# Third stage of a convolution block: quarter-array passes first, then full-row passes, in each chunk

## The chip, the cores and the metric

The kernel runs on one core of one Trainium2 chip. The metric is the device time of one execution in microseconds (us). Five engines work side by side, each through its own instruction list in order: TensorE (PE in the profile; its weight loads are PEld), VectorE (DVE), ScalarE (ACT), GpSimd (POOL) and SyncE (SP). Here SP and POOL mostly issue DMAs. All data is fp32.

## The reference, cut to what matters

The input x is 16 images of 192 channels, 64 x 64 pixels. The work that this change touches is the last third of the first layer:

```python
mixed = gelu(batch_norm((scanned + local) * sigmoid(gate)))     # BN statistics over all images
x  = x + conv1x1(mixed, out_proj_w, out_proj_b)                 # 192 -> 192
h2 = layer_norm_over_channels(x)                                # mean, variance, sqrt(var + 1e-6)
x  = x + conv1x1(gelu(conv1x1(h2, fc1_w, fc1_b)), fc2_w, fc2_b) # 192 -> 768 -> 192
```

Before it come a layer norm, an input projection, a depthwise convolution, and scans in four directions. After it, a second layer averages each image over its pixels, makes 3 x 3 masked depthwise taps from that average (four of the nine are used), and applies them to the image.

## The kernel before

The program has three stages. The first (layer norm and input projection) ends at about 630 us of the span, the second (convolution, scans, batch-norm statistics) at about 1300 us, and the third, which the change is about, takes the rest.

**Tiling of stage three.** Images go in pairs: image 2p on partitions 0 to 63, image 2p + 1 on partitions 64 to 127, so that the 192 channels of both are three tiles t = 0, 1, 2 of 64 channels each. A chunk is 512 pixels (8 rows) of one pair; there are 8 chunks a pair and n_ch = 64 chunks in all. Per chunk the steps are:

- `load`: x of the chunk into one of two buffers `x2s` (SP queue). `load_mixed`: every second chunk, `mixed` into `y_low` (SP queue). `unmix`: three DVE transposes of it into `mxs`. `bn_gelu`: batch norm and GELU on ACT.
- out-projection of tile t: `out_quarters` uses channels 128 to 191 of `mixed`, with quarters of the PE array (64 rows x 64 columns, four matmuls abreast); `out_columns` uses channels 0 to 127 with full rows (128 rows x 64 columns, two abreast). Both add up in one pair of PSUM areas. `residual` (DVE) adds it to x and writes the image `ximg`, and makes the channel sums `sm`.
- layer norm: `mean(n, ..., "sm")` on quarters of the array, `center` (DVE), `squares` (ACT and DVE), `mean(n, ..., "sq")` on quarters, which is the variance, and `normalize`: Sqrt on ACT, reciprocal and multiply on DVE. An ACT table has to be loaded for Sqrt and again for GELU (`warm`).
- `first`: the 192 to 768 product on quarters of the array, six tiles m of 128 outputs, each followed by a GELU on ACT into a `gl` tile. `second`: the 768 to 192 product with full rows (through the helper `both`, so its line in the profile is that of the helper). `final` (DVE) adds it to the image and sums over pixels.
- `piece`: one part of the second layer for the pair before (`dynamic`): one ACT pass, three DVE passes, two output DMAs on the POOL queue. 12 pieces a pair, at most two a chunk. `pooled`, `squeeze` and `excite` compute the taps once a pair.

**Order.** `tc.manual_schedule` keeps each engine's instructions in the order in which the code issues them, so the order of calls is the schedule. A chunk before has three rounds k = 0, 1, 2: `first(n, k)` with two tiles m, then `products(n, k)`, then one `second`. `products(n, t)` puts a mean of chunk n + 1 (t = 0: mean, t = 1: variance) and one tile t of the out-projection of chunk n + 2 into one PSUM tile. On PE a round is therefore: quarters (first, mean, out_quarters), then full rows (out_columns, second).

**PSUM.** Of eight banks, tag "f1" has two buffers of two banks (first, and the out-projection with the means), tag "f2" three buffers of one bank (the three outputs of second), tag "a" one bank.

**Lines of the profile.** L989 is first's matmul and L991 its GELU; L843 is second's matmul (and excite's); L907 is out_quarters, L914 out_columns, L945 mean, L920 residual, L957 center, L964 and L965 squares, L973 to L977 normalize, L1009 final, L1046 and L65 a piece, L870 and L871 bn_gelu, L243 unmix, L1074 a pass of the tail. The end of the kernel (the last pair's second layer) is written out after the loop and shares tags with it (`ol` tiles have the tag "gl").

Of the kernel before, what the change touches and what calls it, by code (L numbers as in the profile page):

```python
# [55 lines left out]
def conv_block_kernel(ctx: ExitStack, tc: tile.TileContext, x, prm, w_in, w_out, w_fc1, b_fc1, w_fc2, w1, bn1, w2, out):  # L56
# [46 lines left out]
    w2t = k2.tile([RED, NTAP, C], F32, tag="w2t", name="w2t")  # L103
    b1 = k2.tile([RED, 4], F32, tag="b1", name="b1")
    s1 = k2.tile([RED, 1], F32, tag="s1", name="s1")
    pv = k2.tile([128, 2, NPRM], F32, tag="pv", name="pv")

    mean64 = k2.tile([128, 64], F32, tag="mean64", name="mean64")

# [55 lines left out]
    SB_ = 2 * 2 * C * BR  # L165
    mid = ce.tile([128, SB_], F32, tag="mid", name="mid")
    ones = ce.tile([128, 128], F32, tag="ones", name="ones")


    bias_g = ce.tile([128, C], F32, tag="bias_g", name="bias_g")  # L170
# [678 lines left out]
    def rows(a):  # L849
        return a.rearrange("p (h w) -> p h w", w=HW)  # L850

    def load(n):
        if n >= 2:
            load_x2(n)
        st[n].update(x2=x2s[n % 2])
# [6 lines left out]
    def unmix(n):  # L862

        for t in range(3 if n else 0):
            turn_back(ys[n // 2], mxs[n % 2], n % 2, t)
        st[n].update(mx=mxs[n % 2])
# [3 lines left out]
        nc.scalar.activation(mx[:, 0:2], mx[:, 0:2], AF.Gelu, bias=bn_bi[:, 0:1], scale=bn_sc[:, 0:1])  # L870
        nc.scalar.activation(mx[:, 2], mx[:, 2], AF.Gelu, bias=bn_bi[:, 1:2], scale=bn_sc[:, 1:2])  # L871

    def products(n, t):


        if not -2 <= n < n_ch - 1:
            return
        ps = ps2.tile([128, 2, CH], F32, tag="f1", name="ps_o", bufs=2)
        pm, po = ps[:, :, HCH:CH], [ps[:, wh, 0:HCH] for wh in range(2)]
        if t < 2:  # L880
            at(mean, n + 1, pm, ("sm", "sq")[t])
        at(out_proj, n + 2, t, po)

        if t == 0:
            at(center, n + 1, pm)
        if t == 1 and 0 <= n + 1 < n_ch:
            st[n + 1]["pw"] = pm
        at(residual, n + 2, t, po)

    cols = lambda a: a.rearrange("p r (k w) -> p r k w", k=2)  # L890

    def out_proj(n, t, ps):
# [6 lines left out]
            out_quarters(n, t, ps, True)  # L899
            out_columns(n, t, ps, False)  # L900

    def out_quarters(n, t, ps, first_):
        s = st[n]

        for wh, qr in enumerate(HALF):
            for i, q in enumerate(HALF):
                nc.tensor.matmul(ps[wh][q], wo2[qr, 64 * t:64 * t + 64], s["mx"][qr, 2, 256 * i:256 * i + 256],  # L907
                                 start=first_, stop=not first_)

    def out_columns(n, t, ps, first_):  # L910
        s = st[n]
        for wh in range(2):
            for i, q in enumerate(HALF):
                nc.tensor.matmul(ps[wh][q].rearrange("p (r w) -> p r w", w=32), wo[:, 64 * t:64 * t + 64],  # L914
                                 cols(rows(s["mx"][:, i]))[:, :, wh], start=first_, stop=not first_)

    def residual(n, t, ps):
        s, img = st[n], img_of(n)
# [20 lines left out]
    def mean(n, ps, what):  # L939


        s0, s1, sx = st[n][what]
        for k, kinds in enumerate(((s0, sx), (sx, s1))):
            for i, a in enumerate(kinds):
                nc.tensor.matmul(ps[HALF[i], k], mean64[HALF[k]], a[HALF[k]], start=True, stop=True)  # L945

    def mean_part(n, pm, t, k, src):

        for i, q in enumerate(HALF):
            nc.tensor.matmul(pm[q, k], mean64[q], src[q], start=(t == 0 and k == 0), stop=(t == 2 and k == 1))  # L950

    def center(n, pm):
        s, img = st[n], img_of(n)
        h = hp2.tile([128, 3, CH], F32, tag="h2", name="h2")
        hr = CR // 2
        for k in range(2):
            nc.vector.tensor_sub(h.rearrange("p t (h w) -> p t h w", w=HW)[:, :, k * hr:(k + 1) * hr], img[:, :, k * hr:(k + 1) * hr],  # L957
                                 rows(pm[:, k]).unsqueeze(1).broadcast_to([128, 3, hr, HW]))
        s.update(h=h)

    def squares(n):
        s = st[n]
        sq = wp.tile([128, 3, CH], F32, tag="sq2", name="sq2")
        nc.scalar.activation(sq, s["h"], AF.Square)  # L964
        nc.vector.tensor_add(sq[:, 0], sq[:, 0], sq[:, 1])  # L965
        v = sq.rearrange("p t (k n) -> p t k n", k=2)
        sums(v[:, 0, 0], v[:, 0, 1], v[:, 1, 0], v[:, 0, 0], v[:, 0, 1], v[:, 2, 0], v[:, 2, 1])
        s.update(sq=(v[:, 0, 0], v[:, 0, 1], v[:, 1, 0]))

    def normalize(n):  # L970
        s = st[n]
        rs = hp2.tile([128, CH], F32, tag="rs2", name="rs2", bufs=1)
        nc.scalar.activation(rs.rearrange("p (k n) -> p k n", k=2), s["pw"], AF.Sqrt, bias=eps6)  # L973

        nc.scalar.activation(warm, eps6, AF.Gelu)
        nc.vector.reciprocal(rs, rs)  # L976
        nc.vector.tensor_mul(s["h"], s["h"], rs.unsqueeze(1).broadcast_to([128, 3, CH]))  # L977

    def first(n, k):

        s = st[n]
        s["gl", k] = []
        for m in (2 * k, 2 * k + 1):
            pf = ps2.tile([128, 2, CH], F32, tag="f1", name="ps_f1", bufs=2)
            for t in range(3):
                for i, q in enumerate(HALF):
                    for j, o in enumerate(HALF):
                        m0 = 128 * m + 64 * j
                        nc.tensor.matmul(pf[o, i], wf1[q, t, m0:m0 + 64], s["h"][q, t], start=(t == 0), stop=(t == 2))  # L989
            gl = wp.tile([128, 2, CH], F32, tag="gl", name="gl", bufs=4)  # L990
            nc.scalar.activation(gl, pf, AF.Gelu, bias=bf1[:, m:m + 1])  # L991
            s["gl", k].append(gl)

    def second(n, k):
        s = st[n]
        if k == 0:
            s["po"] = [ps2.tile([128, CH], F32, tag="f2", name="ps_f2", bufs=3) for _ in range(3)]
        for j, gl in enumerate(s.pop(("gl", k))):
            m = 2 * k + j
            for t in range(3):  # L1000
                both(s["po"][t], lambda i: wf2[:, m, 64 * t:64 * t + 64], lambda i: gl[:, i], m == 0, m == NFC - 1)

# [49 lines left out]
    def dynamic_last(p, r, nr, t, dg, o=None, queues=(nc.gpsimd, nc.sync)):  # L1052
# [11 lines left out]
                nc.sync.dma_start(ov[2 * p + i, 64 * t:64 * t + 64, r * HW:(r + nr) * HW], o[HALF[i]].rearrange("p h w -> p (h w)"))  # L1064
            return

        o = wp.tile([128, GR, HW], F32, tag="gl", name="ol", bufs=4)
        ps = ps2.tile([128, 2, CH], F32, tag="f1", name="ps_d", bufs=2)[:, :, 0:hr * HW]
        for k in range(NTAP):
            for i, q in enumerate(HALF):  # L1070
# [10 lines left out]
    def at(f, n, *a):  # L1081
        if n is not None and 0 <= n < n_ch:
            f(n, *a)
# [3 lines left out]
    def piece():  # L1087
        if pieces:
            dynamic(*pieces.pop(0))

    def out_alone(n, t, later=False):

        if later:
            ps = [ps2.tile([128, CH], F32, tag="f2", name="ps_o2", bufs=3)[:, 0:HCH] for _ in range(2)]
        else:
            pair = ps2.tile([128, 2, CH], F32, tag="f1", name="ps_o", bufs=2)
            ps = [pair[:, wh, 0:HCH] for wh in range(2)]
        out_proj(n, t, ps)
        if not later:
            residual(n, t, ps)  # L1100
        return ps

    def one_bank():
        return ps2.tile([128, 2, HCH], F32, tag="a", name="ps_m")

    def idle(k):

# [20 lines left out]
    for k in range(2):  # L1128
        mean_part(0, pm, 2, k, img0[:, 2, halves[k]])
    center(0, pm)  # L1130
    load(2)
    sq0 = wp.tile([128, 3, CH], F32, tag="sq2", name="sq2").rearrange("p t (k n) -> p k t n", k=2)
    for k in range(2):
        nc.scalar.activation(sq0[:, k], st[0]["h"].rearrange("p t (k n) -> p k t n", k=2)[:, k], AF.Square)
    nc.scalar.activation(warm, eps6, AF.Sqrt)
# [2 lines left out]
    for k in range(2):  # L1138
        for t in range(3):
            mean_part(0, pw, t, k, sq0[:, k, t])  # L1140
    st[0]["pw"] = pw
    normalize(0)
    load_y(4, ys[2], (nc.gpsimd,))
    residual(1, 1, out_alone(1, 1, True))
    out_alone(1, 2)
    idle(1)
    first(0, 0)
    pm = ps2.tile([128, 2, CH], F32, tag="f1", name="ps_o", bufs=2)[:, :, 0:HCH]
    mean(1, pm, "sm")
    unmix(2)  # L1150
    center(1, pm)
    bn_gelu(2)
    squares(1)
    load(3)
    first(0, 1)
    unmix(3)
    out_alone(2, 0)
    second(0, 0)
    bn_gelu(3)
    products(0, 1)  # L1160
    normalize(1)
    first(0, 2)
    products(0, 2)
    second(0, 1)
    nc.vector.memset(pool2, 0.0)

    for n in range(1, n_ch + 1):
        ended = (n - 1) // NCH if n >= NCH and (n - 1) % NCH == NCH - 1 else None
        if n == 1:
            load_y(6, ys[3], (nc.gpsimd,))  # L1170
        if n == NCH - 3:
            border(ximg[1])
        at(load, n + 3)
        at(unmix, n + 3)
        at(load_mixed, n + 4)
        at(first, n, 0)
        at(bn_gelu, n + 3)
        products(n, 0)
        piece()
        at(squares, n + 1)  # L1180
        at(second, n - 1, NPS - 1)
        at(final, n - 1)
        if ended is not None:
            pooled(ended)
            if ended == n_pairs - 1:
                idle(1)
        at(first, n, 1)
        products(n, 1)
        if ended is not None:
            squeeze(ended)  # L1190
        at(second, n, 0)
        piece()
        at(normalize, n + 1)
        at(first, n, 2)
        if ended is not None:
            excite(ended)
            if ended < n_pairs - 1:
                pieces += [(ended, g, t) for g in range(NG) for t in range(3)]
        products(n, 2)
        at(second, n, 1)  # L1200

    last = n_pairs - 1

    def taps_on_diagonals(j):
# [73 lines left out]
```

## Time and profile before

| | us |
|---|---|
| median of 3 runs | 3713.8 (3713.1 to 3716.2) |
| profiled execution | 3712.9 |
| its span, first to last instruction | 3711.1 |
| PE busy | 3689.3 |
| DVE busy | 2702.0 |
| ACT busy | 1782.6 |
| POOL busy | 419.2 |

The profile is of one execution, whose own time lies 1.8 us above its span and 0.9 us below the median. Busy times are summed over the whole span. PE, PEld, DVE, ACT and POOL work side by side, so their times do not add up. A matmul's row in the trace has its true start and a modelled end; PE can look busy while it does not run at its peak. In the groups, `64*64` or `128*64` behind MATMUL is the part of the array (rows times columns) that one instruction takes.

### The profile page before, as it was taken

The page shows a single profiled execution, that of the slowest core. Times are in us where ns is not written, and L with a number is a line of the kernel's source. Part 1 is how long each engine was busy: PE and PEld are TensorE (multiplying, and loading weights), DVE is VectorE, ACT ScalarE, POOL GpSimd, SP SyncE. Part 2 cuts the span into 40 slices and gives each one's busy share as a digit, 9 for nine tenths or more (in the row PEclk, how much of TensorE's full clock was granted, in tenths as well). Part 3 has the DMA queues.
Part 4 walks back from the last instruction along what each step waited for, and adds up shares of the span by engine and source line. Part 5 has one row for each costly group of instructions (what it writes and reads, how often), then busy time and mean ns, then how long its engine had stood idle before and what let it go on. Part 6 is the DMA issues. An engine that isn't in the chain of part 4 may idle for free.

```text
span 3711.1 us, 71206 instructions
## 1 busy us (share of the span) xinstructions
PE 3689.3 (99%) x30354; PEld 1664.0 (45%) x30354; DVE 2702.0 (73%) x4138; ACT 1782.6 (48%) x1940; POOL 419.2 (11%) x685
## 2 busy tenths in 40 slices
PE   9999999999999999999999999999999999999998
PEld 6666666555555533333333333333333333333333
DVE  7878776999999965557656756766675766675764
ACT  3344344888888843334434343434343443443433
POOL 2434342111011020000000000000000000000000
PEclk9999999999999999999999999999999999999999
DMA  7898998999999851112212222222222221221212
GB/s 170 245 255 248 263 276 262 291 297 284 282 281 280 221 101 40 41 44 71 81 51 64 74 61 66 63 66 63 72 57 63 77 67 46 77 75 43 69 38 74
DMA packets 290332, 491.80 MB, mean 133 GB/s; under 512 B 26584, under 2 KB 184784, under 8 KB 290016
## 3 DMA queue, kind: packets, MB, share of 16 engines
q1 hardware_dynamic: 232540, 296.22, 29.7%
q0 software_dynamic: 56544, 189.99, 18.7%
q8 instruction: 240, 3.93, 0.5%
q10 hardware_dynamic: 932, 1.03, 0.1%
q14 instruction: 76, 0.62, 0.1%
HBM read 284.95 MB, written 197.92 MB: 130 GB/s over the span
## 4 chain that ended last, share of the span: by engine, by line
PE 90%; DMA 1%; DVE 1%; ACT 0%; issue 0%; ACTq 0%; SPq 0%; DVEq 0%
PE ps_f L989 27%; PE ps_f L843 27%; PE ps_l L673 11%; PE ps_pj L514 7%; PE ps_d L629 7%; PE ps_o L914 5%; PE ps_o L907 2%; PE ps_o L945 1%; PE ps_xt L485 1%; DMA xa<-in_x_dram 0%; PE ps_k L843 0%; DVE o L65 0%; PE pb_h L142 0%; PE ps_m L950 0%; DMA pg_d<-mid 0%; DVE ol L65 0%
## 5 line engine op out<-in xcount | busy, mean ns | idle before, releaser
L991 ACT ACTIVATE gl<-ps_f,bf 128x1024 f32<-128x1024 f32 x384 | 427.5, 1113 | 1319.5 <-PE ps_f L989 1319.5
L989 PE MATMUL ps_f<-h,wf 64*64 64x512 f32 x9216 | 1033.3, 593 | 3.0 <-DVE h L977 1.9
L843 PE MATMUL ps_f<-gl,place 128*64 128x512 f32 x4608 | 1022.2, 592 | 0.0
L989 PEld LDWEIGHTS ps_f<-h,wf 64*64 64x64 f32 x9216 | 333.6, 133 | 688.4 <-issue 633.7
L843 PEld LDWEIGHTS ps_f<-gl,place 128*64 128x64 f32 x4608 | 334.2, 137 | 574.5 <-issue 533.4
L514 PE MATMUL ps_pj<-wi,xa 64*128 64x384 f32 x3072 | 514.6, 487 | 0.6 <-DVE mid L519 0.3
L957 DVE TENSOR_TENSOR h<-ximg,ps_o 128x768 f32<-128x768 f32 x126 | 114.6, 951 | 420.6 <-PE ps_o L914 412.3
L514 PEld LDWEIGHTS ps_pj<-wi,xa 64*128 64x128 f32 x3072 | 292.0, 187 | 194.7 <-issue 10.6
L920 DVE SCALAR_TENSOR_TENSOR ximg<-ps_o,pt,low 128x256 f32<-128x256 f32 x384 | 167.9, 479 | 262.8 <-PE ps_o L914 260.3
L65 DVE SCALAR_TENSOR_TENSOR o<-ximg,taps,o 128x1024 f32<-128x1024 f32 (+1 forms) x267 | 337.5, 1264 | 11.2 <-ACT o L1046 2.6
L1050 POOL DMA_DIRECT2D out_dram<-o x168 | 89.8, 539 | 2065.7 <-DVE o L65 2062.9
L976 DVE RECIPROCAL rs<-rs 128x512 f32<-128x512 f32 x64 | 214.3, 3349 | 28.6 <-ACT rs L973 28.6
L664 DVE TENSOR_TENSOR_SCAN v<-tab,q 128x1024 f32<-128x1024 f32 x96 | 218.3, 2274 | 6.6 <-ACT tab L652 6.6
L666 DVE TENSOR_TENSOR_SCAN v<-tab,q 128x1024 f32<-128x1024 f32 x96 | 217.5, 2265 | 0.0
L652 ACT ACTIVATE tab<-mask,dec_b 128x1024 f32<-128x1024 f32 x192 | 209.5, 1143 | 0.0
L520 ACT ACTIVATE mid<-ps_pj,rsa 128x384 f32<-128x384 f32 x128 | 120.4, 942 | 183.5 <-PE ps_pj L514 183.5
L914 PE MATMUL ps_o<-low,wo 128*64 128x256 f32 x1536 | 208.1, 392 | 0.0
L520 ACT ACTIVATE stg<-ps_pj,rsa 128x384 f32<-128x384 f32 x128 | 120.2, 941 | 178.9 <-PE ps_pj L514 174.9
L492 DVE BATCH_NORM_STATS2 st<-ps_xt 128x6 f32<-128x192 f32 x512 | 173.3, 339 | 13.2 <-PE ps_xt L485 12.4
L243 DVE STREAM_TRANSPOSE low<-low 128x512 f32<-128x512 f32 x174 | 167.9, 1016 | 2.1 <-issue 0.3
L1009 DVE SCALAR_TENSOR_TENSOR ximg<-ps_f,pt,ximg 128x512 f32<-128x512 f32 x192 | 134.4, 748 | 40.2 <-PE ps_f L843 37.8
L473 POOL DMA_DIRECT2D xa<-in_x_dram x192 | 119.6, 631 | 358.9 <-PE ps_pj L514 317.9
(214 smaller groups left out, 4060.8 us busy)
## 6 DMA issues: line engine op xcount, KB each, us to landing
low<-in_x_dram SPq DMA_DIRECT2D x128, 384.0 KB
out_dram<-o POOLq DMA_DIRECT2D x168, 256.0 KB, 3.7
mid<-pg_d SPq DMA_DIRECT2D x8, 4096.0 KB
low<-mixed_d SPq DMA_DIRECT2D x116, 256.0 KB
low<-pg_d SPq DMA_DIRECT2D x7, 4096.0 KB
pg_o<-pg_d SPq DMA_DIRECT2D x7, 4096.0 KB
xa<-in_x_dram POOLq DMA_DIRECT2D x192, 128.0 KB, 5.5
xa<-in_x_dram SPq DMA_DIRECT2D x192, 128.0 KB
```

The source lines that it names most:

```text
L65: nc.vector.scalar_tensor_tensor(o, in0, scalar, in1, ALU.mult, ALU.add, **kw)
L514: nc.tensor.matmul(ps[i], pixels(n, t, g)[q], wi[q, t].rearrange("p g k c -> p (g k c)"), start=(t == 0), stop=(t == 2))
L520: nc.scalar.activation(stag[blk][1][:, :, j], ps[1], AF.Copy, scale=rs[:, g, 1:2])
L629: nc.tensor.matmul(dst(ps[o, ih]), mats[g % 2]["dm"][q, di + 1, :, ch], src(s["pg"][q, :, 0, ch]), start=(di == 0), stop=stop)
L664: nc.vector.tensor_tensor_scan(vf, tab, q, 0.0, ALU.mult, ALU.add)
L666: nc.vector.tensor_tensor_scan(vf[:, ::-1], tab[:, ::-1], q[:, ::-1], 0.0, ALU.mult, ALU.add)
L673: nc.tensor.matmul(dst(bst[k]["ps"][o, i]), lm_of(g)[q, m, :, c], src(q, ih), start=start, stop=stop)
L843: nc.tensor.matmul(ps[q], w(i), rhs(i), start=start, stop=stop)
L914: nc.tensor.matmul(ps[wh][q].rearrange("p (r w) -> p r w", w=32), wo[:, 64 * t:64 * t + 64], cols(rows(s["mx"][:, i]))[:, :, wh], start=fi ...
L976: nc.vector.reciprocal(rs, rs)
L989: nc.tensor.matmul(pf[o, i], wf1[q, t, m0:m0 + 64], s["h"][q, t], start=(t == 0), stop=(t == 2))
L991: nc.scalar.activation(gl, pf, AF.Gelu, bias=bf1[:, m:m + 1])
```

## The change

In stage three a chunk now has two phases on PE in place of three rounds. First all passes on quarters of the array: first(n, 0) and first(n, 1), the mean of chunk n + 1, first(n, 2) to first(n, 5), out_quarters of chunk n + 2 for t = 0 and 2, the variance of chunk n + 1, out_quarters for t = 1. Then those with full rows: out_columns for the three t, and second with all six tiles.

For this, `first` makes one tile m a call, `gl` has six buffers instead of four, `products` is gone, the out-projection's three outputs lie in two "f1" tiles taken together, and mean and variance take two buffers of "f2" each (so Sqrt is two instructions of 256 columns). `squares` writes into the x2 buffer of its chunk, and so `load` of chunk n + 3 is issued after the variance. `final(n - 1)` comes at the start of a chunk's code, `unmix`, `load_mixed` and the first `piece` behind the first calls, `normalize`, the residuals and `bn_gelu` after out_columns, the second `piece` inside second. `pv` moves to a pool that is closed before stage three.

```diff
-    def products(n, t):
-        if not -2 <= n < n_ch - 1:
-            return
-        ps = ps2.tile([128, 2, CH], F32, tag="f1", name="ps_o", bufs=2)
-        pm, po = ps[:, :, HCH:CH], [ps[:, wh, 0:HCH] for wh in range(2)]
-        if t < 2:
-            at(mean, n + 1, pm, ("sm", "sq")[t])
-        at(out_proj, n + 2, t, po)
-        if t == 0:
-            at(center, n + 1, pm)
-        if t == 1 and 0 <= n + 1 < n_ch:
-            st[n + 1]["pw"] = pm
-        at(residual, n + 2, t, po)
...
     def squares(n):
         s = st[n]
-        sq = wp.tile([128, 3, CH], F32, tag="sq2", name="sq2")
+        sq = x2s[n % 2]
...
-        nc.scalar.activation(rs.rearrange("p (k n) -> p k n", k=2), s["pw"], AF.Sqrt, bias=eps6)
+        for k in range(2):
+            nc.scalar.activation(rs[:, k * HCH:(k + 1) * HCH], s["pw"][k], AF.Sqrt, bias=eps6)
...
+    def two_banks(name):
+        return [ps2.tile([128, CH], F32, tag="f2", name=name, bufs=3)[:, 0:HCH] for _ in range(2)]
...
-    for n in range(1, n_ch + 1):
+    for n in range(n_ch + 1):
         ended = (n - 1) // NCH if n >= NCH and (n - 1) % NCH == NCH - 1 else None
-        at(load, n + 3)
-        at(unmix, n + 3)
-        at(load_mixed, n + 4)
-        at(first, n, 0)
-        at(bn_gelu, n + 3)
-        products(n, 0)
-        piece()
-        at(squares, n + 1)
-        at(second, n - 1, NPS - 1)
         at(final, n - 1)
...
+        at(first, n, 0)
         at(first, n, 1)
-        products(n, 1)
+        if n + 1 < n_ch:
+            pm = two_banks("ps_m")
+            mean(n + 1, pm, "sm")
+            center(n + 1, pm)
...
+        at(first, n, 2)
+        at(squares, n + 1)
+        for m in range(3, NFC):
+            at(first, n, m)
...
+        at(unmix, n + 3)
+        at(load_mixed, n + 4)
+        piece()
+        po = []
+        if n + 2 < n_ch:
+            pair = [ps2.tile([128, 2, CH], F32, tag="f1", name="ps_o", bufs=2) for _ in range(2)]
+            po = [[pair[j][:, wh, c0:c0 + HCH] for wh in range(2)] for j, c0 in ((0, 0), (1, 0), (0, HCH))]
+            for t in (0, 2):
+                out_quarters(n + 2, t, po[t], True, t < 2)
+        if n + 1 < n_ch:
+            st[n + 1]["pw"] = two_banks("ps_v")
+            mean(n + 1, st[n + 1]["pw"], "sq")
+        at(load, n + 3)
+        if n + 2 < n_ch:
+            out_quarters(n + 2, 1, po[1], True)
         if ended is not None:
             squeeze(ended)
+        for t in range(len(po)):
+            out_columns(n + 2, t, po[t], False, t > 0)
+        at(normalize, n + 1)
+        for t in range(len(po)):
+            residual(n + 2, t, po[t])
+        at(bn_gelu, n + 3)
         at(second, n, 0)
-        piece()
-        at(normalize, n + 1)
-        at(first, n, 2)
         if ended is not None:
             excite(ended)
...
-        products(n, 2)
         at(second, n, 1)
+        piece()
+        at(second, n, 2)
```

In the code that starts stage three, the passes that were written out for chunk 0 are now the loop's n = 0; there `unmix(2)` stands behind the first mean and `bn_gelu(2)` behind first(0, 4).

More of the change, by code (lines that the diff above doesn't have):

```diff
@@ L105, in conv_block_kernel @@
     s1 = k2.tile([RED, 1], F32, tag="s1", name="s1")
-    pv = k2.tile([128, 2, NPRM], F32, tag="pv", name="pv")
     mean64 = k2.tile([128, 64], F32, tag="mean64", name="mean64")
@@ L167, in conv_block_kernel @@
     ones = ce.tile([128, 128], F32, tag="ones", name="ones")
+    pv = ce.tile([128, 2, NPRM], F32, tag="pv", name="pv")
     bias_g = ce.tile([128, C], F32, tag="bias_g", name="bias_g")
@@ L900, in out_proj, with out_quarters @@
             out_columns(n, t, ps, False)
-    def out_quarters(n, t, ps, first_):
+    def out_quarters(n, t, ps, first_, start=None):
         s = st[n]
@@ L907, in out_quarters, with out_columns @@
                 nc.tensor.matmul(ps[wh][q], wo2[qr, 64 * t:64 * t + 64], s["mx"][qr, 2, 256 * i:256 * i + 256],
-                                 start=first_, stop=not first_)
-    def out_columns(n, t, ps, first_):
+                                 start=first_ if start is None else start, stop=not first_)
+    def out_columns(n, t, ps, first_, stop=None):
         s = st[n]
@@ L914, in out_columns @@
                 nc.tensor.matmul(ps[wh][q].rearrange("p (r w) -> p r w", w=32), wo[:, 64 * t:64 * t + 64],
-                                 cols(rows(s["mx"][:, i]))[:, :, wh], start=first_, stop=not first_)
+                                 cols(rows(s["mx"][:, i]))[:, :, wh], start=first_, stop=not first_ if stop is None else stop)
     def residual(n, t, ps):
@@ L944, in mean @@
             for i, a in enumerate(kinds):
-                nc.tensor.matmul(ps[HALF[i], k], mean64[HALF[k]], a[HALF[k]], start=True, stop=True)
+                nc.tensor.matmul(ps[k][HALF[i]], mean64[HALF[k]], a[HALF[k]], start=True, stop=True)
     def mean_part(n, pm, t, k, src):
         for i, q in enumerate(HALF):
-            nc.tensor.matmul(pm[q, k], mean64[q], src[q], start=(t == 0 and k == 0), stop=(t == 2 and k == 1))
+            nc.tensor.matmul(pm[k][q], mean64[q], src[q], start=(t == 0 and k == 0), stop=(t == 2 and k == 1))
     def center(n, pm):
@@ L957, in center @@
             nc.vector.tensor_sub(h.rearrange("p t (h w) -> p t h w", w=HW)[:, :, k * hr:(k + 1) * hr], img[:, :, k * hr:(k + 1) * hr],
-                                 rows(pm[:, k]).unsqueeze(1).broadcast_to([128, 3, hr, HW]))
+                                 rows(pm[k]).unsqueeze(1).broadcast_to([128, 3, hr, HW]))
         s.update(h=h)
@@ L977, in normalize, with first @@
         nc.vector.tensor_mul(s["h"], s["h"], rs.unsqueeze(1).broadcast_to([128, 3, CH]))
-    def first(n, k):
+    def first(n, m):
         s = st[n]
[L982 to L992, printed above, removed]
+        pf = ps2.tile([128, 2, CH], F32, tag="f1", name="ps_f1", bufs=2)
+        for t in range(3):
+            for i, q in enumerate(HALF):
+                for j, o in enumerate(HALF):
+                    m0 = 128 * m + 64 * j
+                    nc.tensor.matmul(pf[o, i], wf1[q, t, m0:m0 + 64], s["h"][q, t], start=(t == 0), stop=(t == 2))
+        gl = wp.tile([128, 2, CH], F32, tag="gl", name="gl", bufs=6)
+        nc.scalar.activation(gl, pf, AF.Gelu, bias=bf1[:, m:m + 1])
+        s["gl", m] = gl
     def second(n, k):
@@ L997, in second @@
             s["po"] = [ps2.tile([128, CH], F32, tag="f2", name="ps_f2", bufs=3) for _ in range(3)]
-        for j, gl in enumerate(s.pop(("gl", k))):
-            m = 2 * k + j
+        for m in (2 * k, 2 * k + 1):
+            gl = s.pop(("gl", m))
             for t in range(3):
@@ L1065, in dynamic_last @@
             return
-        o = wp.tile([128, GR, HW], F32, tag="gl", name="ol", bufs=4)
+        o = wp.tile([128, GR, HW], F32, tag="gl", name="ol", bufs=6)
         ps = ps2.tile([128, 2, CH], F32, tag="f1", name="ps_d", bufs=2)[:, :, 0:hr * HW]
@@ L1093, in out_alone @@
         if later:
-            ps = [ps2.tile([128, CH], F32, tag="f2", name="ps_o2", bufs=3)[:, 0:HCH] for _ in range(2)]
+            ps = two_banks("ps_o2")
         else:
@@ L1103, in one_bank @@
     def one_bank():
-        return ps2.tile([128, 2, HCH], F32, tag="a", name="ps_m")
+        ps = ps2.tile([128, 2, HCH], F32, tag="a", name="ps_m")
+        return [ps[:, k] for k in range(2)]
+    def two_banks(name):
+        return [ps2.tile([128, CH], F32, tag="f2", name=name, bufs=3)[:, 0:HCH] for _ in range(2)]
     def idle(k):
@@ L1130, in conv_block_kernel @@
     center(0, pm)
-    load(2)
-    sq0 = wp.tile([128, 3, CH], F32, tag="sq2", name="sq2").rearrange("p t (k n) -> p k t n", k=2)
+    sq0 = x2s[0].rearrange("p t (k n) -> p k t n", k=2)
     for k in range(2):
@@ L1141, in conv_block_kernel @@
     st[0]["pw"] = pw
+    load(2)
     normalize(0)
@@ L1146, in conv_block_kernel @@
     idle(1)
[L1147 to L1165, printed above, removed]
-    for n in range(1, n_ch + 1):
-        ended = (n - 1) // NCH if n >= NCH and (n - 1) % NCH == NCH - 1 else None
[L1169 to L1172, printed above, removed]
-        at(load, n + 3)
-        at(unmix, n + 3)
-        at(load_mixed, n + 4)
-        at(first, n, 0)
-        at(bn_gelu, n + 3)
-        products(n, 0)
-        piece()
-        at(squares, n + 1)
-        at(second, n - 1, NPS - 1)
+    for n in range(n_ch + 1):
+        ended = (n - 1) // NCH if n >= NCH and (n - 1) % NCH == NCH - 1 else None
         at(final, n - 1)
@@ L1186, in conv_block_kernel @@
                 idle(1)
-        at(first, n, 1)
-        products(n, 1)
+        if n == 0:
+            nc.vector.memset(pool2, 0.0)
+        if n == 1:
+            load_y(6, ys[3], (nc.gpsimd,))
+        if n == NCH - 3:
+            border(ximg[1])
+        at(first, n, 0)
+        at(first, n, 1)
+        if n + 1 < n_ch:
+            pm = two_banks("ps_m")
+            mean(n + 1, pm, "sm")
+            center(n + 1, pm)
+        if n == 0:
+            unmix(2)
+        at(first, n, 2)
+        at(squares, n + 1)
+        for m in range(3, NFC):
+            at(first, n, m)
+            if n == 0 and m == 4:
+                bn_gelu(2)
+        at(unmix, n + 3)
[13 more added lines that the diff above has]
+            out_quarters(n + 2, 1, po[1], True)
         if ended is not None:
             squeeze(ended)
+        for t in range(len(po)):
[4 more added lines that the diff above has]
+        at(bn_gelu, n + 3)
         at(second, n, 0)
-        piece()
-        at(normalize, n + 1)
-        at(first, n, 2)
         if ended is not None:
```

## The prediction

> **What bounds the kernel now.** I read the page first: busy times, the slices, the groups.
>
> ```profile
> span 3711.1 us, 71206 instructions
> PE 3689.3 (99%) x30354; PEld 1664.0 (45%) x30354; DVE 2702.0 (73%) x4138; ACT 1782.6 (48%) x1940; POOL 419.2 (11%) x685
> PEclk9999999999999999999999999999999999999999
> L976 DVE RECIPROCAL rs<-rs 128x512 f32<-128x512 f32 x64 | 214.3, 3349 | 28.6 <-ACT rs L973 28.6
> ```
>
> PE is busy all the time at full clock, DVE has a quarter free. But "busy" is not "at its peak", so the second view is the PE timeline of one chunk in the middle of stage three, with a first() block at both ends:
>
> ```profile
> 2303.43 5.38 PE L989 MATMUL ps_f<-h,wf 64*64 64x512 f32 x48
> 2308.63 0.61 PE L907 MATMUL ps_o<-low,wo 64*64 64x256 f32 x8
> 2309.17 1.08 PE L914 MATMUL ps_o<-low,wo 128*64 128x256 f32 x8
> 2310.08 5.32 PE L843 MATMUL ps_f<-gl,place 128*64 128x512 f32 x24
> 2315.33 5.38 PE L989 MATMUL ps_f<-h,wf 64*64 64x512 f32 x48
> 2320.53 0.61 PE L945 MATMUL ps_o<-sm,mean 64*64 64x256 f32 x8
> 2320.96 0.61 PE L907 MATMUL ps_o<-low,wo 64*64 64x256 f32 x8
> 2321.51 1.08 PE L914 MATMUL ps_o<-low,wo 128*64 128x256 f32 x8
> 2322.42 5.32 PE L843 MATMUL ps_f<-gl,place 128*64 128x512 f32 x24
> 2327.67 5.38 PE L989 MATMUL ps_f<-h,wf 64*64 64x512 f32 x48
> ...
> 2340.01 2.38 PE L989 MATMUL ps_f<-h,wf 64*64 64x512 f32 x20
> ```
>
> Columns: start, duration, engine, line, operation, tiles, rows\*columns of the array, count. Only the starts matter (ends are modelled). Four 64\*64 matmuls run abreast, or two 128\*64. In the weight-load rows of the first block, ten steps take 2303.91 to 2308.20: 0.429 us for a group of 512 columns; a group of 256 takes half, 0.215 (L945 to L907, two groups: 0.43). No block waits for data: the view of waits, for PE alone between 1400 and 3640 us, is empty. What the reader is to see is where the starts are later than the columns explain. L945 to L907, both 64\*64: nothing lost. L907 to L914, 64\*64 to 128\*64: 0.55 instead of 0.43. L914 to L843, both 128\*64: 0.91 instead of 0.86, 0.05 lost (in finer time behind its first pair, so it is the tail of the change before). L843 to L989, back: 5.25 instead of 5.15, and the L989 block itself 5.20. So a round trip from quarters to full rows and back loses about 0.12 + 0.05 + 0.10 + 0.05 = 0.32. Check on the whole chunk: 2303.43 to 2340.01 is 36.58 us; columns are 72 groups of 512 (30.91) and 22 of 256 (4.74), 35.65. The rest, 0.93, over three round trips is 0.31 each. I use 0.31.
>
> **The change, part by part.** *Round trips.* Each of the 64 chunks now has one in place of three: quarters for first(), both means and out_quarters, then full rows for out_columns and second(). Two saved: 2 x 0.31 x 64 = **-39.7 us**. The Trainium skill, "TensorEngine Tiling (Array Packing)", Key Properties, says that changing the tiling mode drains the array, without a price; "TensorE: Matmul & The Clock Gate", Single matmul latency, has 398 cycles at 2.4 GHz of fixed latency, 0.166 us. Two such drains are 0.33 a round trip, and the sum -42.5. The row's 0.31 stands.
>
> *A new wait.* Call T the start of the first matmul behind first(n, 5). The pair of PSUM tiles for the out-projection takes the buffers of the last two first() tiles, so pair 0 (t = 0, 2) is free once GELU 4 has read it, pair 1 (t = 1) only after GELU 5. Ahead of t = 1 stand 6 groups of 256 (t = 0, t = 2, variance): T + 1.29. The same wait is in the trace once, in the prologue, where first(0, 1) takes the buffer of the tile just filled:
>
> ```profile
> 1331.35 0.61 PE L945 MATMUL ps_o<-sm,mean 64*64 64x256 f32 x8
> 1332.77 1.52 PE L989 MATMUL ps_f<-h,wf 64*64 64x512 f32 x12 [0.80 <-ACT gl L991]
> ```
>
> Here the buffer came 1.42 after the following matmul's start. So t = 1 starts at T + 1.42, 0.13 late, plus 0.05 for a first group without weights preloaded (as behind a change): 0.18 x 62 chunks that have an out-projection = **+11.2**. All that is queued behind it on PE (out_columns, second) shifts with it. Bounds: 0 if GELU 5 is early, 1.47 if the wait came at the pair's first matmul (rival C).
>
> *Sqrt in two halves and second().* The variance moves to two banks of tag f2, and second(n, 0) needs these for its t = 1 and t = 2. New: PE waits for ACT there.
>
> ```profile
> 2333.18 1.11 ACT L991 ACTIVATE gl<-ps_f,bf 128x1024 f32<-128x1024 f32 x1 [1.46 <-PE ps_f L989]
> 2334.19 1.23 ACT L1046 ACTIVATE o<-ximg,pt,taps 128x1024 f32<-128x1024 f32 x1
> 2335.93 1.28 ACT L973 ACT_TABLE_LOAD   x1 [0.51 <-DVE ximg L920]
> 2337.22 0.69 ACT L973 ACTIVATE rs<-ps_o,eps 128x512 f32<-128x512 f32 x1
> ```
>
> ACT from T: GELU 5 starts at 0.30 (2308.63 to 2308.93 above the same), the piece's pass 1.01 later at 1.31, ends 2.54; table load 1.28, to 3.83; Sqrt of 256 columns is 0.69 less 256 columns at 0.83 ns (1.11 for 1024, 0.69 for 512), 0.48 each: done at 4.31 and 4.80. PE: t = 1 quarters 1.47 to 1.90, change 0.16, 12 pairs of columns 2.59, so second() starts at 4.65, its t = 1 at 5.08, its t = 2 at 5.51. Margins 0.7 and 0.65: cost 0. The skill speaks against this: "ScalarE: Activation LUTs", What ACT_TABLE_LOAD costs, gives 1.28 us for the load (agrees) and a drain of about 1.38 behind it. Here the Sqrt starts 1.29 after its load, no drain in the row. With the page's 1.38 the Sqrt would be 0.74 too late in the 42 chunks whose first piece() has work (without it ACT is 1.2 ahead): +31, and nearly nothing would be left of the gain. I take the row: 0.
>
> *DVE order.* From T in a chunk with two pieces: scalar_tensor_tensors 2.6 to 6.5 (3.92 for three), reciprocal and multiply 3.35 and 1.76 to 11.6, three residuals with their sums (0.88 x 3, 0.69, 1.78) to 16.7, second piece to 20.6, final() (three of 0.75) to 22.9. PE ends second() and starts the next first() at T + 20.25: h is 8.6 us early, the residuals free the pair 5 us early. mean of "sm" takes two f2 banks of final(): needed at T + 20.25 + 5.15 = 25.4, 2.5 spare. Squares: center, Square (1.47) and sums (2.5) end 13.5 after first(n, 0)'s start, needed at 16.7. Cost 0; uncovered, a late DVE costs PE its lateness, each 0.1 us a chunk 6 us.
>
> *Buffers and queues.* squares now writes x2's buffer, so the load of chunk n + 3 (two DMAs of 384 KB on SP) is issued after the variance matmul, T + 1.3, not at the chunk's start. Its reader is the residual at the next T + 12, 48 us later; before it was under 40, and no wait for it shows. On SP it stands behind the eight DMAs of load_mixed, which wait only for the unmix done at about T + 0.5, and ahead of the next chunk's. POOL's queue keeps its order. 0.
>
> *Small terms.* excite() is quarters (48\*64) and now sits between full-row blocks: 7 x 0.31 = **+2.2**. Chunk 0: the 0.99 us shown above (1.42 less 0.43) and a stall of 0.55 (a first() block's halves start at 1346.71 and 1349.84, 3.13 apart where six groups take 2.58) go, but bn_gelu(2) holds back the quarters by about 0.8: **-0.8**. Split Sqrt on the prologue's path: **+0.2**. Tail: six "gl" buffers for four; one ACT pass there waits:
>
> ```profile
> 3701.22 1.11 ACT L1074 ACTIVATE ol<-ps_d,pt 128x1024 f32<-128x1024 f32 x1 [4.41 <-DMA out_dram<-ol]
> ```
>
> It sits right behind ACT's own DMA issue (3699.83 to 3701.02), so most stays: between 0 and -4, I take **-1**.
>
> Sum: -39.7 + 11.2 + 2.2 - 0.8 + 0.2 - 1 = **-27.9**. The profiled execution took 3712.9 (span 3711.1), so 3685.0; the median, 0.9 higher, gives **3686**.
>
> **The rivals.** *B, Sqrt late.* second() waits for the variance banks. Its place: the second and third pair of second(n, 0). It starts to cost from 0.65 us of delay on ACT and eats the whole gain at 1.3. With the drain of 1.38 above: 3686 + 31 = 3717, no change. Against it: the row of 1.29.
>
> *C, slower.* The release of the out-projection's buffers comes at the pair's first matmul, not tile by tile: t = 0 then waits for GELU 5, 1.47 a chunk instead of 0.18, 62 x 1.29 = +80, 3766. It decides from 0.45 us more a chunk. For it: both tiles are taken together. Against: second(n, 0) takes three tiles together too, and a weight-load row at 2336.05, well inside its block that began at 2334.76, names DVE as what it waited for last; so waits do stand at later matmuls of such a block.
>
> *D, no saving.* The lost 0.31 is tied to something else than the array's shape; then the new wait stays and little else: about 3713.8 + 12 = 3726. Against: two boundaries of the same shape lose nothing, every boundary of different shapes does.
>
> *E, more.* GELU 5 in time and the tail's 4 us: 3686 - 11 - 3 = 3672.
>
> **How the numbers follow.** The computed case 0.75 (own range 3678 to 3694), E 0.08, B or a smaller DVE wait 0.11 (3694 to 3717), C 0.04, D 0.02. The range 3670 to 3702 takes in E and half of B. A measurement here tells 0.2% (7.4 us) from no change: faster is the computed case, E and over half of B, 0.89; same 0.05; slower 0.06.
>
> **What would show it.** Right: one chunk of about 36.1 us from first() to first(); PE blocks of 64\*64 unbroken up to the third out_quarters; a wait of PE on ACT gl of about 0.1 us once a chunk; no wait on rs; second() unbroken. Wrong: waits of PE on ACT rs (B) or on DVE ximg, or over 1 us before the first out_quarters (C); a chunk with one change of shape that still loses 0.9 (D).

## The result and the profile after

The changed kernel takes 3697.0 us (median of 5 runs, 3695.6 to 3699.5) against 3713.1 us; the ratio is 0.9957, 95% interval 0.9942 to 0.9972. A second comparison on one chip (run e2 below) gave 3696.7 against 3715.3, ratio 0.9948, 0.9935 to 0.9960. The change makes the kernel faster by 16 to 19 us. The forecast was 3686, range 3670 to 3702: right in sign and range, but 28 us of gain were forecast. The rest of this document is about where the other ten or so went.

The page of the changed kernel first:

```profile
span 3697.7 us, 71384 instructions
PE 3670.5 (99%) x30354; PEld 1715.5 (46%) x30354; DVE 2705.5 (73%) x4138; ACT 1791.1 (48%) x2004; POOL 420.6 (11%) x685
PEclk9999999999999999999999999999999999999999
L961 DVE RECIPROCAL rs<-rs 128x512 f32<-128x512 f32 x64 | 214.3, 3349 | 53.5 <-ACT rs L958 53.5
```

Every share is as before, within a point: PE has 30354 matmuls again, DVE and ACT the same work (64 more instructions on ACT, the halved Sqrt). The last row shows DVE waiting 53.5 us in all for Sqrt in place of 28.6, which costs nothing, as its product `h` is ready long before PE needs it (below). Busy shares could not have told that 20 us of PE time could be had. The PE timeline of one chunk in the middle tells it (columns: start, duration, engine, line, operation, tiles, rows\*columns of the array, count):

```profile
2316.83 5.38 PE L972 MATMUL ps_f<-h,wf 64*64 64x512 f32 x48
2322.03 0.61 PE L928 MATMUL ps_m<-sm,mean 64*64 64x256 f32 x8
2322.46 10.48 PE L972 MATMUL ps_f<-h,wf 64*64 64x512 f32 x96
2332.76 1.04 PE L890 MATMUL ps_o<-low,wo 64*64 64x256 f32 x16
2333.62 0.61 PE L928 MATMUL ps_v<-low,mean 64*64 64x256 f32 x8
2334.24 0.66 PE L890 MATMUL ps_o<-low,wo 64*64 64x256 f32 x8
2334.83 2.81 PE L897 MATMUL ps_o<-low,wo 128*64 128x256 f32 x24
2337.47 15.62 PE L843 MATMUL ps_f<-gl,place 128*64 128x512 f32 x72
2353.02 1.07 PE L972 MATMUL ps_f<-h,wf 64*64 64x512 f32 x5
```

From first() to first() 36.19 us, before 36.58. The shape changes once (64\*64 to 128\*64 at 2334.83) and back once. Six blocks of quarters follow each other without loss but for one step: from the variance at 2333.62 to out_quarters at 2334.24 it is 0.62 in place of 0.43. The view of weight loads names the reason:

```profile
2334.23 0.21 PEld L890 LDWEIGHTS ps_o<-low,wo 64*64 64x64 f32 x8 [0.45 <-ACT gl L974]
```

This is the forecast wait for GELU 5. After it the block takes 0.59 to the next in place of 0.54 (in e7 below, behind the same wait, 0.48 in place of 0.43).

The total, split at two rows of the PE timeline, the start of first(0, 0) and the start of the block behind the last second():

| us | before | after |
|---|---|---|
| start to first(0, 0) | 1326.15 | 1333.21 |
| chunk loop, to 3672.09 and 3659.07 | 2345.9 | 2325.9 |
| rest, to the end of the span | 39.0 | 38.6 |
| span | 3711.1 | 3697.7 |

The loop is 20.1 us shorter, and 7 us of that are lost ahead of it. The change does little there: it moves `pv`, issues the load of chunk 2 later, and halves the Sqrt just before first(0, 0), whose wait for `h` is 2.01 us in place of 1.85.

### The profile page after: what moved, and what is told of

It is laid out like the page before. It is cut to its first block, busy times and chain, and to the rows that moved or that the text cites. A ratio compares the mean times of both kernels' runs of the same rounds, so it can differ in the third digit from the quotient of the medians.

```text
span 3697.7 us, 71384 instructions
## 1 busy us (share of the span) xinstructions
PE 3670.5 (99%) x30354; PEld 1715.5 (46%) x30354; DVE 2705.5 (73%) x4138; ACT 1791.1 (48%) x2004; POOL 420.6 (11%) x685
## 4 chain that ended last, share of the span: by engine, by line
PE 98%; DMA 1%; DVE 1%; issue 0%; ACT 0%; SPq 0%; ACTq 0%; POOL 0%
PE ps_f L972 27%; PE ps_f L843 27%; PE ps_pj L514 14%; PE ps_l L673 11%; PE ps_d L629 7%; PE ps_o L897 5%; PE ps_o L890 3%; PE ps_xt L485 2%; PE ps_m L928 1%; PE ps_v L928 1%; DMA xa<-in_x_dram 1%; PE ps_k L843 0%; DVE o L65 0%; PE pb_h L141 0%; DVE ol L65 0%
## 5 line engine op out<-in xcount | busy, mean ns | idle before, releaser
L972 PE MATMUL ps_f<-h,wf 64*64 64x512 f32 x9216 | 1014.9, 590 | 2.0 <-DVE h L962 2.0
L843 PE MATMUL ps_f<-gl,place 128*64 128x512 f32 x4608 | 1003.6, 593 | 2.8 <-ACT rs L958 2.8
L972 PEld LDWEIGHTS ps_f<-h,wf 64*64 64x64 f32 x9216 | 346.3, 133 | 627.9 <-issue 566.0
L940 DVE TENSOR_TENSOR h<-ximg,ps_m 128x768 f32<-128x768 f32 x128 | 116.4, 951 | 264.6 <-PE ps_m L928 263.4
L961 DVE RECIPROCAL rs<-rs 128x512 f32<-128x512 f32 x64 | 214.3, 3349 | 53.5 <-ACT rs L958 53.5
L949 DVE TENSOR_TENSOR low<-low 128x512 f32<-128x512 f32 x63 | 43.6, 693 | 209.2 <-ACT low L948 209.2
L897 PE MATMUL ps_o<-low,wo 128*64 128x256 f32 x1536 | 181.8, 384 | 0.0
```

Of the source, the lines that this page charges most:

```text
L843: nc.tensor.matmul(ps[q], w(i), rhs(i), start=start, stop=stop)
```

## Experiments

**The stretch ahead of the loop: e1, e2, e3.** e1 is the kernel before, e2 the changed kernel, both unchanged; e3 is the kernel before with one edit of the change:

```diff
-    pv = k2.tile([128, 2, NPRM], F32, tag="pv", name="pv")
...
     ones = ce.tile([128, 128], F32, tag="ones", name="ones")
+    pv = ce.tile([128, 2, NPRM], F32, tag="pv", name="pv")
```

> The kernel before, unchanged, as the yardstick for the stretch ahead of stage three's chunk loop. In the two first profiles this stretch (start to first(0, 0)) was 1326.2 us before and 1333.2 after, although only one small tile (pv) was moved there. Theory S (scatter: starting phase, granted clock and DMA arrival in stage one differ from run to run): another profile of the same kernel gives another value, some us away from 1326.2, and a loop of 2345.9 within 0.3. Theory P (the moved tile pv shifts the buffers behind it and stage one gets slower): 1326 again within 1 us. Total 3713 within 0.1%.

> The changed kernel, unchanged. Both theories: loop from first(0, 0) to the end of the last second() 2325.9 within 0.3, so 20.1 us shorter than before. Theory S: the stretch ahead of it scatters around the same mean as that of the kernel before, total about 3693 to 3697. Theory P: the stretch is again about 1331 to 1333, total about 3697.

> The kernel before with one edit of the change alone: pv moved to the early pool. Theory S: no difference from before, 3713 within 0.1%, stretch ahead of the loop in the scatter of the others. Theory P: 4 us slower than before, about 3717, all of it ahead of the loop.

Measured: e3 3715.3 us against 3715.3 for before (ratio 1.0000, 0.9992 to 1.0009), so the move of `pv` costs nothing in the median. The profiles have the stretch ahead of first(0, 0) at 1328.7 (e1), 1331.5 (e3) and 1329.0 (e2), besides 1326.2 and 1333.2 above: it scatters by some us, in either kernel, and the changed kernel has had a shorter one (e2) than the kernel before with `pv` moved (e3). The loop hardly scatters: 2345.9 in e1, 2325.9 in e2; e3 has 2347.6, and all of that 1.7 lies between the starts of first(0, 0) and first(0, 1), 8.31 apart there and 6.62 in before. The granted clock in that block is 0.59 in e3 (1331 to 1335 us) and 1.00 in before (1326 to 1330 us); chunk 62, below, shows the same.

Where does the scatter arise? Two answers of the view by stretches, for the first 100 us of before and of after (us, then busy PE, PEld, DVE, ACT, POOL, then the granted clock, DMA share, GB/s):

```profile
0.00:100.00 100.00, 96.45 (x620) 65.32 (x622) 70.33 (x236) 36.40 (x49) 32.52 (x60) 1.00 0.70 167
```

```profile
0.00:100.00 100.00, 94.77 (x599) 63.10 (x600) 68.89 (x230) 35.70 (x48) 29.55 (x55) 0.97 0.67 160
```

In the second the granted clock was 0.97 and 599 matmuls were done in place of 620, a loss of some 3 us, made early, before any changed line. Split at the first matmul of the second stage (L629), all profiles so far, and that of e4 below, read:

| | clock in the first 100 us | matmuls there | start of stage two | start of first(0, 0) |
|---|---|---|---|---|
| before | 1.00 | 620 | 632.2 | 1326.2 |
| e1 | 1.00 | 624 | 633.3 | 1328.7 |
| e3 | 0.97 | 600 | 636.6 | 1331.5 |
| after | 0.97 | 599 | 638.1 | 1333.2 |
| e2 | 1.00 | 618 | 634.4 | 1329.0 |
| e4 | 0.98 | 610 | 630.0 | 1324.4 |

From stage two to first(0, 0) all six take 694.0 to 695.4; the first stage alone spreads by 8 us. Theory S stands and theory P falls. The clock of the first 100 us is a part of the scatter only: e4, with 0.98, has the shortest first stage. What sets the rest stays open.

**Is it the array's shape? e5, e6.** Both add one matmul of 64 columns a chunk between first(n, 3) and first(n, 4), whose product is not used; they differ in the rows that it takes:

```diff
+            if m == 3 and n < n_ch:
+                pi = ps2.tile([128, CH], F32, tag="a", name="ps_i")
+                nc.tensor.matmul(pi[0:64, 0:64], wo[:, 0:64], ident[:, 0:64], start=True, stop=True)       # e5
+                nc.tensor.matmul(pi[0:64, 0:64], wo[0:64, 0:64], ident[0:64, 0:64], start=True, stop=True) # e6
```

> The changed kernel with one more matmul a chunk, of 64 columns with full rows (128 rows x 64 columns of the array) into the idle PSUM bank, in the middle of the quarter phase between first(n, 3) and first(n, 4); its product is not used. Theory A (the lost time belongs to the change of array shape): it costs its own columns, some 0.03 to 0.06 us, and a round trip of 0.31: 64 x 0.31 = 20 more than the same with a quarter matmul, so about 3696.7 + 20 + 3 = 3720. Theory D (the lost time belongs to a new block, new weights and a new output, whatever its shape): the same as the quarter version within 3 us.

> The same extra matmul of 64 columns at the same place into the same bank, but on a quarter of the array (64 rows x 64 columns); its product is not used. Theory A: no round trip, only its own columns: 0.03 to 0.06 a chunk, 3698 to 3701. Theory D: as much as the full-row version, about 3720.

PE timelines of e5 and then e6 around the extra matmul (L1163):

```profile
2331.24 5.33 PE L972 MATMUL ps_f<-h,wf 64*64 64x512 f32 x48
2336.50 0.33 PE L1163 MATMUL ps_i<-ident,wo 128*64 128x64 f32 x2
2336.76 5.38 PE L972 MATMUL ps_f<-h,wf 64*64 64x512 f32 x48
2341.96 1.04 PE L890 MATMUL ps_o<-low,wo 64*64 64x256 f32 x16
```

```profile
2323.69 5.33 PE L972 MATMUL ps_f<-h,wf 64*64 64x512 f32 x48
2328.84 0.22 PE L1163 MATMUL ps_i<-ident,wo 64*64 64x64 f32 x1
2328.84 0.65 PE L972 MATMUL ps_f<-h,wf 64*64 64x512 f32 x3
2328.89 0.22 PE L1163 MATMUL ps_i<-ident,wo 64*64 64x64 f32 x1
2328.95 5.31 PE L972 MATMUL ps_f<-h,wf 64*64 64x512 f32 x45
2334.04 1.08 PE L890 MATMUL ps_o<-low,wo 64*64 64x256 f32 x16
```

From the first() block to out_quarters e5 takes 10.72 and e6 10.35, against 10.30 without. The chunk, from first() to first(), is 36.61 in e5 (2325.61 to 2362.22) and, from mean to mean, 36.30 in e6 (2323.26 to 2359.56): 0.31 apart for the same 64 columns. (At the place itself they are 0.37 apart; e6 then loses 0.06 of its lead, as its wait for GELU 5 is longer: 0.67 from the variance to out_quarters, where e5 has 0.61.) The medians are 3721.5 and 3704.2 us, 17 apart, the loops 2351.0 and 2333.3; 64 x 0.31 would be 20, and most of the other 2 lies in chunk 62, where the granted clock fell in e6 and not in e5 (shown under e4). e6 came out 3 us above the end that was expected, for the 0.06 just named. Theory A stands: the time goes with the change of shape; a new block, a new output bank and new weights of the same shape cost next to nothing beyond their columns. One such round trip put back into each chunk, with 7 us for the small matmul itself (e6's loop against 2325.9), takes back the whole gain (e5 against before: 1.0015, 1.0006 to 1.0024).

**The wait for GELU 5: e7.**

```diff
+        if n + 2 < n_ch:
+            out_quarters(n + 2, 1, po[1], True)
         if n + 1 < n_ch:
             st[n + 1]["pw"] = two_banks("ps_v")
             mean(n + 1, st[n + 1]["pw"], "sq")
         at(load, n + 3)
-        if n + 2 < n_ch:
-            out_quarters(n + 2, 1, po[1], True)
```

> The changed kernel with one exchange: out_quarters for t = 1 stands ahead of the variance, so 4 groups of 256 (0.86 us) instead of 6 (1.29) lie between the end of first(n, 5) and the first matmul that needs GELU 5's buffer. Theory G (that matmul waits for GELU 5, which ends 1.42 us after first(n, 5)'s last group): the wait grows by 0.43, steady chunk 36.19 + 0.43 = 36.62, 62 x 0.43 = 26.7, 3723. Rival (the 0.18 lost ahead of t = 1 belongs to the variance matmul or to the step between the two): chunk and time unchanged, 3697.

PE timeline of e7:

```profile
2340.96 1.04 PE L890 MATMUL ps_o<-low,wo 64*64 64x256 f32 x16
2342.44 0.66 PE L890 MATMUL ps_o<-low,wo 64*64 64x256 f32 x8 [0.43 <-ACT gl L974]
2342.92 0.61 PE L928 MATMUL ps_v<-low,mean 64*64 64x256 f32 x8
```

The waiting matmul stands again 1.48 behind T (2340.96 to 2342.44; 2332.76 to 2334.24 in the changed kernel), whatever lies between, and the chunk is 36.62 (2325.03 to 2361.65), as forecast. 3721.9 us, ratio to before 1.0017 (1.0010 to 1.0023): this order of two calls turns the gain into a small loss. Theory G stands.

**Two repairs: e4.**

```diff
         if n + 1 < n_ch:
-            st[n + 1]["pw"] = two_banks("ps_v")
+            if n + 2 < n_ch:
+                st[n + 1]["pw"] = two_banks("ps_v")
+            else:
+                last_pair = ps2.tile([128, 2, CH], F32, tag="f1", name="ps_o", bufs=2)
+                st[n + 1]["pw"] = [last_pair[:, k, 0:HCH] for k in range(2)]
...
         at(load_mixed, n + 4)
+        if n % NCH == NCH - 2:
+            piece()
         piece()
...
         at(second, n, 0)
-        if ended is not None:
-            excite(ended)
-            if ended < n_pairs - 1:
-                pieces += [(ended, g, t) for g in range(NG) for t in range(3)]
         at(second, n, 1)
         piece()
         at(second, n, 2)
+        if ended is not None:
+            excite(ended)
+            if ended < n_pairs - 1:
+                pieces += [(ended, g, t) for g in range(NG) for t in range(3)]
```

> The changed kernel with two repairs. (1) excite is issued after second(n, 2), at the border of full rows and quarters, in place of after second(n, 0), and one piece of each pair is moved to the chunk with n % 8 = 6. (2) In chunk 62, which has no out-projection to stand between the variance and second(), the variance goes to an f1 tile, so second() does not wait for its Sqrt. My theory: chunks with excite lose 1.90 - 1.24 = 0.66 less, 7 x 0.66 = 4.6, and chunk 62 loses its 2.8 us wait of PE on ACT rs: 7.4 in the loop, 3697.0 - 7.4 = 3689.6. Rival: excite's extra time is a wait for its 24 small products and not the two changes of array shape; then only the 2.8 comes, 3694.

Measured: 3686.5 us (3684.3 to 3689.6), ratio to before 0.9922 (0.9909 to 0.9934), faster than both kernels; e2 on the same chip 3696.7. The loop is 2319.3, 6.6 shorter than the changed kernel's; the other 3.5 of the 10 between the medians lie outside it, where the stretch ahead of it scatters (1324.4 in this profile); for the medians themselves the split is not shown. The 6.6 are not divided as I expected. Chunk 62 gave 4.7 and excite 1.7 (0.24 for each of seven). For excite I had misread the profile of before: its two long rounds there, 12.62 and 13.30, stand in place of 12.34 and 11.91, so excite and squeeze cost 1.67 before, not 1.24, 1.90 after and 1.66 in e4. So the extra 0.24, somewhat less than a round trip of 0.31, is gone. Chunk 62 shows more than a wait. PE timeline of the changed kernel, then the same chunk in e4:

```profile
3607.03 0.61 PE L928 MATMUL ps_v<-low,mean 64*64 64x256 f32 x8
3607.57 1.08 PE L843 MATMUL ps_f<-gl,place 128*64 128x512 f32 x4
3611.42 16.51 PE L843 MATMUL ps_f<-gl,place 128*64 128x512 f32 x68 [2.77 <-ACT rs L958]
3627.86 4.52 PE L972 MATMUL ps_f<-h,wf 64*64 64x512 f32 x40
```

```profile
3596.84 15.67 PE L843 MATMUL ps_f<-gl,place 128*64 128x512 f32 x72
3612.44 4.09 PE L972 MATMUL ps_f<-h,wf 64*64 64x512 f32 x36
```

With no out-projection between variance and second(), PE has nothing to do while ACT ends GELU 5, a piece, the table load and Sqrt. Second()'s block takes 20.29 in place of 15.60. Its second tile should start 0.05 + 0.86 behind 3607.57 and starts at 3611.42, 2.9 late. The other 1.7 come after the wait; the stretches of the changed kernel show from what:

```profile
3608.00:3611.00 3.00, 0.65 (x4) 0.00 (x0) 1.35 (x2) 2.97 (x4) 0.00 (x0) 1.00 0.00 0
...
3612.00:3616.00 4.00, 4.00 (x14) 1.17 (x12) 3.96 (x3) 1.24 (x2) 1.07 (x2) 0.57 0.28 60
3616.00:3620.00 4.00, 4.00 (x20) 1.29 (x18) 2.56 (x2) 0.00 (x0) 0.00 (x0) 1.00 0.23 71
```

The granted clock (third number from the end) is 0.57 in the four us after the wait, and 14 matmuls are done where the next four us have 20. But the same wait does not always bring this. In e5, whose chunk 62 has the same calls around it, the second row below stands in place of the 0.57, and the block is 1.70 shorter (14.81 for 16.51):

```profile
3635.30 14.81 PE L843 MATMUL ps_f<-gl,place 128*64 128x512 f32 x68 [2.77 <-ACT rs L958]
```

```profile
3636.00:3640.00 4.00, 4.00 (x20) 1.29 (x18) 3.96 (x3) 1.11 (x2) 1.07 (x2) 1.00 0.30 66
```

So chunk 62 costs 3.0 in e5 and e7 (no fall of the clock) and 4.7 in after, e2 and e6 (0.57 to 0.61 over four us). Of e4's 4.7, then, 3.0 is the wait that it removes, and 1.7 is a fall of the clock that some executions do not have. In e3 the same loss of 1.7 followed PE's wait of 1.85 us ahead of first(0, 0), which the other profiles show without such a loss. The Trainium skill, "TensorE: Matmul & The Clock Gate", Part 1 (the HAM clock gate), says that an idle window of about 3.4 us halves the clock until the array has been busy for as long, and that these windows run freely. The size agrees: at half clock, 0.57 over four us is 3.4 us of it. The length does not: PE stood for some 3 us (2.77 by the row), and for less in e3, and the clock fell in some executions and not in others. Free-running windows would make it a matter of chance, but no run here shows them.

## Why the prediction was right, and where its size was off

- **Round trips: right.** 0.31 was read from one chunk; e5 against e6 gives 0.31 for one that is put in by itself. The row's price stands. The 0.33 set beside it was an estimate from the Trainium skill, "TensorE: Matmul & The Clock Gate", Single matmul latency, whose figure is for a single bf16 matmul, while this kernel is fp32; that it comes near does not show that the loss is such a drain. The runs show that the time goes with the change of shape, not what the array does in it.
- **The wait for GELU 5: right in place and cause, too small.** Forecast 0.13 + 0.05, measured 0.05 more: the steady chunk is 36.19, forecast 36.14. The row used, from the prologue, had the next matmul start 1.42 behind the mean, as the GELU there began 0.25 behind it (1331.60 after 1331.35); in the loop GELU 5 begins 0.31 behind T (2333.07), ends at T + 1.42 and lets the matmul start at T + 1.48. The 0.30 that the prediction itself read for GELU 5 in the chunk of before would have given 1.47. 62 x 0.05 is 3 us.
- **Sqrt in halves: right for 62 chunks, missed for one.** ACT of the changed kernel:

```profile
2333.07 1.11 ACT L974 ACTIVATE gl<-ps_f,bf 128x1024 f32<-128x1024 f32 x1 [1.46 <-PE ps_f L972]
2334.08 1.23 ACT L1029 ACTIVATE o<-ximg,pt,taps 128x1024 f32<-128x1024 f32 x1
2335.33 1.28 ACT L958 ACT_TABLE_LOAD   x1
2336.62 0.84 ACT L958 ACTIVATE rs<-ps_v,eps 128x256 f32<-128x256 f32 x2
```

  Both halves are done at T + 4.70 (forecast 4.80), and Sqrt starts 1.29 behind the start of its table load: the drain of about 1.38 of the skill's "ScalarE: Activation LUTs", What ACT_TABLE_LOAD costs, which would have taken nearly all of the gain, is not there. Nor is it ahead of the load, which starts 0.02 behind the end of the piece's pass. Spare was even more than computed: the 24 matmuls of a third of second() are six tiles of four, so t = 1 starts 0.86 behind t = 0 and not 0.43. But the cost of 0 was worked out for the chunk with out_columns as cover, and the one chunk without it was left out. There the cover is gone: +3.0 for the wait, and +1.7 where the clock fell behind it.
- **DVE order: right.** h ready at 2344.33, T + 11.6 as forecast, 8.7 us ahead of the next first(); final() ends at 2355.1, T + 22.4 (22.9), 3.1 us ahead of the mean that takes its banks at 2358.22.
- **Load later: right**, the views of waits list none for it on PE or DVE in the loop.
- **excite: right**, +1.7 for +2.2. **Tail: no gain shown.** 38.6, 40.0 (e2) and 39.8 (e4) against 39.0 and 38.8: six buffers did not shorten it.
- **The sum.** Forecast for the loop: -39.7 + 11.2 + 2.2 - 0.8 = -27.1; measured -20.1. The terms that were mis-sized: +3 (GELU 5), +4.7 (chunk 62; 1.7 of it not in every execution), -0.5 (excite), together 7.2 for a difference of 7.0. Outside the loop, the halved Sqrt of the prologue came as forecast (0.16 for 0.2), and the tail gave nothing for 1. What lies between -20.1 in the loop and -16 or -19 in the medians is most likely the scatter of the first stage, which the sum had no term for; it is shown for the profiled executions alone. So 3697 lies above the computed case's own range (up to 3694), in the part that the range took in for B; what B describes gave at most 4.7 us of it, in one chunk. That the total still fell into the range owes something to its width.
- **Rivals.** C and D fell (in the timeline of the chunk the wait stands at the third out_quarters alone; e5 and e6 show that the shape is what counts). B's mechanism exists, but in one chunk alone. E did not happen: GELU 5 was later than computed, and the tail gained nothing.

## What to carry to other kernels

When PE looks fully busy, compare the starts of its blocks with the columns they move: time that is lost where two neighbours use the array in different shapes (0.31 us a round trip here) comes back if passes of one shape are gathered. Each gathering moves some eviction to where the next phase needs its buffer, so order the passes inside a phase to put as much work as possible behind the last eviction. And cost a hidden wait for the first and last trips of a loop too: the trip that lacks the covering work paid 3.0 to 4.7 us.

## What the runs showed of the hardware that was not expected

A wait of some 3 us on PE was followed by a granted clock of 0.57 to 0.61 over the next four us in three of five profiles, at a loss of another 1.7 us; in the other two the same wait left the clock at 1.00. A wait of 1.85 us did the same in one profile (e3). And the first stage of an unchanged program scatters by several us between profiles (in two profiles of the changed kernel it ends at 638.1 and 634.4), with the granted clock of its first 100 us between 0.97 and 1.00.
